# Where the gates of an interleaved scan are computed: in each group's own scan, or all ahead in the first

## The chip, the cores and the metric

The kernel runs on one core of one Trainium2 chip. A core has five engines that follow their own instruction streams: TensorE (PE in the profile, with its weight loads shown apart as PEld), VectorE (DVE), ScalarE (ACT), GpSimd (POOL) and SyncE (SP), which here only issues DMAs. The metric is the device time of one execution in microseconds (us). Lower is better. A profiled execution gives the trace; its span runs from the first to the last instruction.

## The reference, cut to what matters

The input `x` is 32 sequences of 256 tokens and 256 features. A gated state-space block (`_L0_cond_ref`) is followed by two layers of windowed attention with feed-forward (`_L0_ffn_ref`), and the input is added at the end. The change is in the first block:

```python
xr, gate = jnp.split(x @ W_in.T, 2, axis=-1)          # 512 channels each
xr = xr + t_emb[:, None, :]
xc = silu(conv4(xr) + b_conv)
xn = layernorm(xc) * ln_g + ln_b
Bm, Cm, dt = jnp.split(xn @ W_xproj.T, 3, axis=-1)
...
def step(h, inputs):                                    # one token after the other
    ad, bd, xt, ct = inputs
    h = jnp.clip(h * ad[:, :, None] + bd[:, :, None] * xt[:, None, :], -10.0, 10.0)
    return h, jnp.einsum('bd,bdh->bh', ct, h)
...
y = ys + D * xn
cond = y * jax.nn.silu(gate) @ W_out.T
...
out = x + ffn(cond)
```

All arithmetic is in float32.

## The kernel before

**Groups and slots.** The 32 sequences are four groups of 8 (`g` = 0 to 3 in the code; "groups 2 to 4" are `g` = 1 to 3). One group's scan is 256 steps, one per token, for all 8 sequences at once: a state tile `h` of 128 partitions (16 states x 8 sequences) by 512 channels is updated by one VectorE instruction (line 716). The scan is cut into 8 chunks of 32 steps (`c`, `CH` = 32). Work around the steps is put into numbered slots, one slot per step: `at(s, f, ...)` says that `f` is recorded in slot `s`, and `s0` is the first slot of a chunk. `scan_slots` runs through the slots and records what stands there. The scan of group `g` has the slots from 256·g on, so group 1 of the code is recorded right behind group 0.

**What runs with what.** The first scan (`alone`, `g` = 0) has the machine to itself. From slot 274 on, attention and feed-forward of group 0 are recorded, stage by stage, with the scan of group 1 between their stages, and so on: attention of group `g` runs beside the scan of group `g`+1. Attention and feed-forward of the last group run with no scan beside them. The tile framework builds the engines' instruction streams from the recorded order, its own estimates and the buffers that are free; each engine then runs its stream in order.

**One chunk of a scan.** `project` multiplies the chunk's inputs with `W_in`: one PSUM tile per 128 channels, two matmuls each (`KM` = 2 halves of the 256 features). Channels 0 to 3 are the convolution's inputs, channels `NC_` + 0 to 3 are the gates. For `g` = 0, `load_x` (line 452) loads the inputs and `project` (line 395, matmuls on line 399) makes all eight. For the later groups the four convolution inputs were made during the first scan: `ahead_load`, `ahead_project`, `ahead_copy`, `ahead_put` (lines 410 to 443) take 48 units `u`, each two of the channel tiles of one chunk, multiply, copy from PSUM on ScalarE and store to DRAM; `load_projected` (line 445) loads them back. Their gates were not: `load_x` and `project` run for them in each later scan, at slots `s0`+6 and `s0`+13 to `s0`+18.

**The gates.** `gate_th` (line 760) brings a gate tile from PSUM to SBUF in the order that the output needs (`reorder`, line 369). In the first scan it applies SiLU directly. In the later ones it copies, then takes tanh of half the value (line 768), and `gate_out` (line 771) forms (1 + tanh)·gate on VectorE, which is twice the SiLU. The factor is taken out by `halve` (line 327), which halves `W_out` once, and by `copy_y` (line 817), which doubles the first group's output. `out_gate` (line 790) multiplies with the gates at slots `s0`+25 and `s0`+41; `project_y` (line 805) applies `W_out`.

**The rows.** A step needs its token's normalised row on all 16 states, scaled per partition. `load_rows` (line 682) fetches it by a DMA that repeats the row 16 times from DRAM (`xrep<-xnd`, 256 KB), into one of 6 buffers, six slots ahead; `scale_row` (line 702) scales it on ScalarE two slots ahead. In the first scan some rows come from TensorE instead: `spread_rows` (line 687) makes two rows from `xq` by two matmuls that contract 32 partitions each, into two PSUM tiles (`bx`), and `scale_row` reads those. `by_tensor` (line 679) says which: with `NQ` = 4 and `XR` = 2, two rows of eight.

**Queues and buffers.** SP issues nearly all DMAs, in the recorded order. All PSUM tiles (`bank`) share 8 banks. The line numbers below are those of the kernel before.

Of the kernel before, what the change touches and what calls it, by code (L numbers as in the profile page):

```python
# [10 lines left out]
FP = mybir.dt.float32  # L11
BF = mybir.dt.bfloat16
I32 = mybir.dt.int32
AF = mybir.ActivationFunctionType
ALU = mybir.AluOpType
# [4 lines left out]
P = 128  # L20
# [6 lines left out]
GB = 8  # L27
# [46 lines left out]
def kernel(  # L74
# [147 lines left out]
    def program(ctx, exact):  # L222
# [14 lines left out]
        def constants(at):  # L237
# [88 lines left out]

            def halve():


                tc.keep_in_program_order(  # L330
                    nc.gpsimd.tensor_scalar_mul(w_out_sb, w_out_sb, 0.5)
                )

            def load_tables():
# [28 lines left out]
            at(-16, load_later)  # L363
            at(14, halve)
            at(30, load_tables)
# [11 lines left out]
        def group_scan(g):  # L377
# [32 lines left out]
            def ahead_load(u):  # L410
                if u % 2 == 0:
                    gg, c = 1 + u // 2 // NCH, u // 2 % NCH
                    t = ap_.tile([P, KM, GB, CH], FP, tag="rot", name="xa", bufs=4)
                    for k in range(KM):
                        nc.sync.dma_start(
                            out=t[:, k],
                            in_=xT[:, k, gg * GB : (gg + 1) * GB, c * CH : (c + 1) * CH],
                        )
                    state["xa", u // 2] = t

            def ahead_project(u):
                ps = bank(ps_w, "w", "ps_a").rearrange("p (r n) -> p r n", r=2)
                for r in range(2):
                    ch = 2 * (u % 2) + r
                    for k in range(KM):
                        nc.tensor.matmul(
                            ps[:, r],
                            w_in_sb[:, k, ch * P : (ch + 1) * P],
                            state["xa", u // 2][:, k],
                            start=(k == 0),  # L430
                            stop=(k == KM - 1),
                        )
                state["pa", u] = ps

            def ahead_copy(u):
                t = aw.tile([P, 2, GB * CH], FP, tag="pT", name="xs_a", bufs=6)
                nc.scalar.copy(t, state.pop(("pa", u)))
                state["ta", u] = t
# [6 lines left out]
            def load_projected(c, i):  # L445
                t = sp.tile([P, 2, GB * CH], FP, tag="xg", name="xp", bufs=2)
                nc.sync.dma_start(out=t, in_=projected[((g - 1) * NCH + c) * 2 + i])
                for r in range(2):
                    ck[c]["ps", 2 * i + r] = t[:, r]


            def load_x(c):
# [226 lines left out]
            def by_tensor(t):  # L679
                return alone and t % (2 * NQ) < XR  # L680

# [78 lines left out]
            def gate_th(c, ch):  # L760
                if ch == 0:
                    ck[c]["sg"] = sp.tile([P, NC_, GB * CH], FP, tag="sg", name="sg")
                sg = ck[c]["sg"][:, ch]
                reorder(sg, ck[c].pop(("ps", NC_ + ch)), AF.Silu if alone else AF.Copy)
                if alone:
                    return
                th = sp.tile([P, GB * CH], FP, tag="th", name="th_g", bufs=2)
                nc.scalar.activation(th, sg, AF.Tanh, scale=0.5)
                ck[c]["th_g", ch] = th

            def gate_out(c, ch):
                sg = ck[c]["sg"][:, ch]
                nc.vector.scalar_tensor_tensor(
                    sg, ck[c].pop(("th_g", ch)), 1.0, sg, ALU.add, ALU.mult
                )

# [40 lines left out]
            def copy_y(c, d):  # L817
# [6 lines left out]
                    AF.Copy,  # L824
                    scale=2.0 if alone else 1.0,
                )
# [29 lines left out]
            for c in range(NCH):  # L856
# [8 lines left out]
                for ch in range(NC_):  # L865
# [3 lines left out]
                    if not alone:  # L869
                        at(s0 - 35 + 2 * ch, conv_out, c, ch)  # L870
                for ch, s in enumerate((13, 16, 17, 18)):
                    at(s0 + s + 2, gate_th, c, ch)
                    if not alone:
                        at(s0 + s + 4, gate_out, c, ch)
                at(s0 - 25, raw_copy, c)
# [19 lines left out]
            for c in range(NCH):  # L895
                s0 = c * CH
                at(s0 - 43 if alone else s0 + 6, load_x, c)
                if alone:
                    for ch in range(NC_):
                        at(s0 - 40 + 2 * ch, project, c, ch)  # L900
                else:
                    for i in range(2):
                        at(s0 - 44 + 2 * i, load_projected, c, i)
                for ch, s in enumerate((13, 16, 17, 18)):
                    at(s0 + s, project, c, NC_ + ch)
                at(s0 - 27, raw_sums, c)
# [16 lines left out]
            if alone:  # L923
                n = (NG - 1) * NCH * 2
                for u in range(n):
                    s = -30 + u * (NCH * CH) // n
                    at(s - 5, ahead_load, u)
                    at(s, ahead_project, u)
                    at(s + 2, ahead_copy, u)
                    at(s + 4, ahead_put, u)  # L930
# [731 lines left out]
```

## Time and profile before

| What | Value |
|---|---|
| Median of three runs | 3590.94 us (3585.17 to 3603.19) |
| The profiled execution, its own time | 3582.75 us |
| Its span, first to last instruction | 3581.0 us |
| Busy share of the span | PE 96%, PEld 63%, DVE 74%, ACT 56%, POOL 53% |
| First step of the first scan (VectorE, line 716) | 47.53 us |
| Start of the second scan (line 836, second instruction) | 435.98 us |
| Mean granted clock of TensorE | 0.992 |
| DMA | 435.68 MB, 122 GB/s over the span |

Busy time is the time in which an engine executes at least one instruction. TensorE's matmuls overlap one another and their ends are modelled, so its busy time is not its work: two views are needed, how long it is busy and how closely instructions follow each other. A float32 matmul of the program appears as two records in the trace. A row of a group reads: line, engine, operation, tiles written and read, shapes, number of records, then busy us and mean ns of one, then the engine's idle time just before them and what ended it. A row of the windows view has the stretch, its length, then busy us and (number of instructions) for PE, PEld, DVE, ACT and POOL, the granted clock, the DMA engines' busy share and GB/s.

### The profile page before, as it was taken

The page shows a single profiled execution, that of the slowest core. Times are in us where ns is not written, and L with a number is a line of the kernel's source. Part 1 is how long each engine was busy: PE and PEld are TensorE (multiplying, and loading weights), DVE is VectorE, ACT ScalarE, POOL GpSimd, SP SyncE. Part 2 cuts the span into 40 slices and gives each one's busy share as a digit, 9 for nine tenths or more (in the row PEclk, how much of TensorE's full clock was granted, in tenths as well). Part 3 has the DMA queues.
Part 4 walks back from the last instruction along what each step waited for, and adds up shares of the span by engine and source line. Part 5 has one row for each costly group of instructions (what it writes and reads, how often), then busy time and mean ns, then how long its engine had stood idle before and what let it go on. Part 6 is the DMA issues. An engine that isn't in the chain of part 4 may idle for free.

```text
span 3581.0 us, 57673 instructions
## 1 busy us (share of the span) xinstructions
PE 3446.0 (96%) x20220; PEld 2253.9 (63%) x20220; DVE 2667.3 (74%) x5049; ACT 1998.7 (56%) x3599; POOL 1892.2 (53%) x1842
## 2 busy tenths in 40 slices
PE   7999989999999999999999999999999999999999
PEld 4555335666656666666666666666666677777777
DVE  5888889888788777888787778888877555555553
ACT  4666656656555665566566655655666444434442
POOL 4433477645556555655565556555544454544551
PEclk9999999999999999999999999999999999999999
DMA  7887665445354545444454555534454112011101
GB/s 207 219 221 213 198 174 149 120 117 143 109 144 125 149 141 148 130 118 127 118 142 125 138 149 140 143 106 131 114 141 122 54 50 61 13 30 38 33 27 37
DMA packets 468767, 435.68 MB, mean 122 GB/s; under 512 B 228723, under 2 KB 308084, under 8 KB 468340
## 3 DMA queue, kind: packets, MB, share of 16 engines
q1 hardware_dynamic: 384018, 419.88, 42.0%
q10 hardware_dynamic: 84450, 12.01, 2.0%
q8 instruction: 163, 2.67, 0.3%
q14 instruction: 136, 1.11, 0.1%
HBM read 383.54 MB, written 46.66 MB: 120 GB/s over the span
## 4 chain that ended last, share of the span: by engine, by line
PE 61%; DVE 19%; DMA 7%; POOL 6%; ACT 4%; issue 3%; SPq 0%; ACTq 0%; DVEq 0%; POOLq 0%
PE ps_qkv L989 13%; PE pa L1375 13%; DVE h L716 7%; PE po_f L1402 7%; DMA xrep<-xnd 5%; PE ps_wo L1039 5%; PE y L728 4%; PE ov L1271 4%; PE sc L1215 3%; PE ps_out L808 3%; PE ps_in L399 2%; PE tr_qk L1028 2%; PE rs L1252 2%; ACT xrep L706 2%; DVE acc L489 2%
## 5 line engine op out<-in xcount | busy, mean ns | idle before, releaser
L716 DVE CUSTOM_DVE_ANT_0 h<-h,xrep,lim 128x512 f32<-128x512 f32 x1024 | 961.0, 938 | 228.9 <-ACT xrep L706 196.6
L706 ACT ACTIVATE xrep<-xrep,beta 128x512 f32<-128x512 f32 x960 | 672.3, 718 | 341.4 <-DMA xrep<-xnd 219.8
L989 PE MATMUL ps_qkv<-qkv,res 128*128 128x512 f32 x1536 | 713.5, 601 | 17.9 <-DVE rinv L1260 8.4
L1375 PE MATMUL pa<-hT,w 128*128 128x256 f32 (+1 forms) x2816 | 675.1, 382 | 11.3 <-DVE zT L799 10.7
L1375 PEld LDWEIGHTS pa<-hT,w 128*128 128x128 f32 (+1 forms) x2816 | 516.9, 188 | 152.9 <-issue 35.4
L1013 POOL TENSOR_TENSOR rot<-rot,swp 128x512 f32<-128x512 f32 x256 | 339.9, 1328 | 475.3 <-DVE swp L1010 423.5
L1021 POOL TENSOR_TENSOR rn<-ss,neg_half 128x8 f32<-128x8 f32 x256 | 466.8, 1823 | 18.4 <-DVE ss L1019 7.8
L989 PEld LDWEIGHTS ps_qkv<-qkv,res 128*128 128x128 f32 x1536 | 282.2, 191 | 301.6 <-issue 241.4
L728 PE MATMUL y<-h,ly 128*32 128x512 f32 x2048 | 348.9, 609 | 16.9 <-DVE h L716 13.9
L1327 POOL TENSOR_TENSOR rstd<-ve,neg_half 128x2 f32<-128x2 f32 x64 | 46.9, 733 | 527.6 <-DVE ve L1325 511.3
L1393 DVE SCALAR_TENSOR_TENSOR ag<-pa,b_sb,ag 128x256 f32<-128x256 f32 x320 | 151.6, 474 | 222.4 <-ACT ag L1386 222.3
L1402 PE MATMUL po_f<-ag,w 128*128 128x256 f32 x1280 | 309.0, 389 | 5.9 <-DVE fo L1413 3.8
L1022 POOL TENSOR_TENSOR rot<-rot,rn 128x512 f32<-128x512 f32 x256 | 289.4, 1130 | 20.0
L1402 PEld LDWEIGHTS po_f<-ag,w 128*128 128x128 f32 x1280 | 236.8, 191 | 71.3 <-issue 12.0
L1386 ACT ACTIVATE ag<-pa,b_sb 128x256 f32<-128x256 f32 x320 | 150.2, 469 | 233.1 <-PE pa L1375 232.1
L1002 ACT ACTIVATE sq<-ps_qkv 128x512 f32<-128x512 f32 x256 | 150.8, 595 | 185.1 <-PE ps_qkv L989 119.4
L1039 PE MATMUL ps_wo<-oT,wo 128*128 128x256 f32 x1024 | 231.7, 379 | 0.5 <-DVE ag L1393 0.5
L489 DVE SCALAR_TENSOR_TENSOR acc<-xr,wc_sb,acc 128x256 f32<-128x256 f32 x384 | 195.1, 531 | 47.7 <-POOL acc L478 47.2
L1005 DVE TENSOR_TENSOR rot<-ps_qkv,rc_sb 128x512 f32<-128x512 f32 x256 | 174.8, 683 | 65.6 <-ACT sq L1002 65.0
L1039 PEld LDWEIGHTS ps_wo<-oT,wo 128*128 128x128 f32 x1024 | 194.4, 190 | 28.1 <-DVE ag L1393 0.9
L1227 ACT ACTIVATE pT<-sc 128x512 f32<-128x512 f32 x384 | 202.3, 603 | 7.6 <-PE sc L1215 5.8
L1271 PE MATMUL ov<-pT,v_sb 128*64 128x256 f32 (+1 forms) x2048 | 183.7, 330 | 19.4 <-DVE ag L1393 19.3
(160 smaller groups left out, 5482.8 us busy)
## 6 DMA issues: line engine op xcount, KB each, us to landing
xrep<-xnd SPq DMA_DIRECT2D x960, 256.0 KB
rb<-inv SPq DMA_DIRECT2D x128, 256.0 KB
xnd<-xn SPq DMA_DIRECT2D x64, 256.0 KB
qkv<-in_wqkv_dram SPq DMA_DIRECT2D x24, 512.0 KB
ahead<-xs_a SPq DMA_DIRECT2D x48, 256.0 KB
xp<-ahead SPq DMA_DIRECT2D x48, 256.0 KB
xd<-xnd SPq DMA_DIRECT2D x192, 64.0 KB
w<-in_w_dram SPq DMA_DIRECT2D x80, 128.0 KB
```

The costliest lines, as they stand in the source:

```text
L489: nc.vector.scalar_tensor_tensor(acc, xr[:, :, k : k + CH], wc_sb[:, ch, k : k + 1], acc, ALU.mult, ALU.add,)
L706: scaled = nc.scalar.activation(bx, ck[c].pop(("bx", t), bx), AF.Copy, scale=ck[c]["beta"][:, t : t + 1])
L716: nc.vector._custom_dve(TENSOR_ADD_SAT, out=h_new, in0=state["h"], in1=bx, s0=ck[c]["lim"][:, 0, t : t + 1], s1=ck[c]["lim"][:, 1, t : t + 1],
L728: nc.tensor.matmul(ck[c]["y", hb][32 * q : 32 * q + 32, :], ly[hb % 2][:, 32 * t : 32 * t + 32], ck[c].pop(("h", hb * TB + t)), start=(i = ...
L989: nc.tensor.matmul(ps, res[b][:, k, t0 : t0 + W], wt["qkv", a][:, k], start=(k == 0), stop=(k == KM - 1),)
L1013: nc.gpsimd.tensor_add(rot, rot, swp)
L1021: nc.gpsimd.tensor_tensor(rn, ss, neg_half, ALU.pow)
L1022: nc.gpsimd.tensor_mul(rot, rot, bc(rn, 2, DH))
L1039: nc.tensor.matmul(po[:, d], wt["wo", 0][:, c, d * P : (d + 1) * P], oT[:, c, :], start=(c == 0), stop=(c == NC_ - 1),)
L1271: nc.tensor.matmul(ov[r * DH : (r + 1) * DH, i, kw * W :], self.qkv[b][2][:, kw, h * DH : (h + 1) * DH], self.p.pop((b, kw, i0 + i, r)), s ...
L1375: nc.tensor.matmul(dst[x], wt["w1", m][:, k, x], self.h[:, k], start=(k == 0), stop=(k == KM - 1),)
L1402: nc.tensor.matmul(self.po[:, d], wt["w2", 0][:, m, d * P : (d + 1) * P], self.ag[m], start=(m == 0), stop=(m == len(MCH) - 1),)
```

## The change

The gates of groups 2 to 4 are made in the first scan as well. The units of `ahead_*` become 96: for each chunk two units of convolution inputs, as before, and two of gates, which are brought from PSUM by two SiLU instructions with the new order instead of one copy. They are stored in the same way, and `load_gates` loads them at slot `s0`+15. The units begin at slot −14 and spread over 276 slots (before: 48 units from slot −30 over 256). `load_x`, the gates' `project`, `gate_th` and `gate_out` are gone from the later scans; `halve` and the factor in `copy_y` are gone too. `by_tensor` now takes two rows of every four.

```diff
-            def halve():
-                tc.keep_in_program_order(
-                    nc.gpsimd.tensor_scalar_mul(w_out_sb, w_out_sb, 0.5)
-                )
...
-            at(14, halve)
...
             def ahead_load(u):
-                if u % 2 == 0:
-                    gg, c = 1 + u // 2 // NCH, u // 2 % NCH
+                if u % 4 == 0:
+                    gg, c = 1 + u // 4 // NCH, u // 4 % NCH
...
             def ahead_project(u):
...
-                    ch = 2 * (u % 2) + r
+                    ch = 2 * (u % 4) + r
...
             def ahead_copy(u):
                 t = aw.tile([P, 2, GB * CH], FP, tag="pT", name="xs_a", bufs=6)
-                nc.scalar.copy(t, state.pop(("pa", u)))
+                ps = state.pop(("pa", u))
+                if u % 4 < 2:
+                    nc.scalar.copy(t, ps)
+                else:
+                    for r in range(2):
+                        reorder(t[:, r], ps[:, r], AF.Silu)
                 state["ta", u] = t
...
-                nc.sync.dma_start(out=t, in_=projected[((g - 1) * NCH + c) * 2 + i])
+                nc.sync.dma_start(out=t, in_=projected[((g - 1) * NCH + c) * 4 + i])
...
+            def load_gates(c):
+                sg = ck[c]["sg"] = sp.tile([P, NC_, GB * CH], FP, tag="sg", name="sg")
+                for i in range(2):
+                    nc.sync.dma_start(
+                        out=sg[:, 2 * i : 2 * i + 2],
+                        in_=projected[((g - 1) * NCH + c) * 4 + 2 + i],
+                    )
...
             def by_tensor(t):
-                return alone and t % (2 * NQ) < XR
+                return alone and t % NQ < XR
...
-                sg = ck[c]["sg"][:, ch]
-                reorder(sg, ck[c].pop(("ps", NC_ + ch)), AF.Silu if alone else AF.Copy)
-                if alone:
-                    return
-                th = sp.tile([P, GB * CH], FP, tag="th", name="th_g", bufs=2)
-                nc.scalar.activation(th, sg, AF.Tanh, scale=0.5)
-                ck[c]["th_g", ch] = th
-
-            def gate_out(c, ch):
-                sg = ck[c]["sg"][:, ch]
-                nc.vector.scalar_tensor_tensor(
-                    sg, ck[c].pop(("th_g", ch)), 1.0, sg, ALU.add, ALU.mult
-                )
+                reorder(ck[c]["sg"][:, ch], ck[c].pop(("ps", NC_ + ch)), AF.Silu)
...
-                    scale=2.0 if alone else 1.0,
...
-                at(s0 - 43 if alone else s0 + 6, load_x, c)
                 if alone:
+                    at(s0 - 43, load_x, c)
...
+                    for ch, s in enumerate((13, 16, 17, 18)):
+                        at(s0 + s, project, c, NC_ + ch)
                 else:
                     for i in range(2):
                         at(s0 - 44 + 2 * i, load_projected, c, i)
-                for ch, s in enumerate((13, 16, 17, 18)):
-                    at(s0 + s, project, c, NC_ + ch)
+                    at(s0 + 15, load_gates, c)
...
-                n = (NG - 1) * NCH * 2
+                n = (NG - 1) * NCH * 4
                 for u in range(n):
-                    s = -30 + u * (NCH * CH) // n
+                    s = -14 + u * 276 // n
                     at(s - 5, ahead_load, u)
                     at(s, ahead_project, u)
                     at(s + 2, ahead_copy, u)
                     at(s + 4, ahead_put, u)
```

More of the change, by code (lines that the diff above doesn't have):

```diff
@@ L418, in ahead_load @@
                         )
-                    state["xa", u // 2] = t
+                    state["xa", u // 4] = t
             def ahead_project(u):
@@ L428, in ahead_project @@
                             w_in_sb[:, k, ch * P : (ch + 1) * P],
-                            state["xa", u // 2][:, k],
+                            state["xa", u // 4][:, k],
                             start=(k == 0),
@@ L870, in group_scan @@
                         at(s0 - 35 + 2 * ch, conv_out, c, ch)
-                for ch, s in enumerate((13, 16, 17, 18)):
-                    at(s0 + s + 2, gate_th, c, ch)
-                    if not alone:
-                        at(s0 + s + 4, gate_out, c, ch)
+                if alone:
+                    for ch, s in enumerate((13, 16, 17, 18)):
+                        at(s0 + s + 2, gate_th, c, ch)
                 at(s0 - 25, raw_copy, c)
@@ L896, in group_scan @@
                 s0 = c * CH
-                at(s0 - 43 if alone else s0 + 6, load_x, c)
                 if alone:
+                    at(s0 - 43, load_x, c)
                     for ch in range(NC_):
                         at(s0 - 40 + 2 * ch, project, c, ch)
+                    for ch, s in enumerate((13, 16, 17, 18)):
+                        at(s0 + s, project, c, NC_ + ch)
                 else:
@@ L903, in group_scan @@
                         at(s0 - 44 + 2 * i, load_projected, c, i)
-                for ch, s in enumerate((13, 16, 17, 18)):
-                    at(s0 + s, project, c, NC_ + ch)
+                    at(s0 + 15, load_gates, c)
                 at(s0 - 27, raw_sums, c)
```

## The prediction

> **What bounds the kernel now.** I read the windows view first, by stage: four middle chunks of the first scan, the stage in which attention runs beside a scan, and the last stage, in which no scan is left.
>
> ```profile
> core 0: us, PE busy (x) PEld busy (x) DVE busy (x) ACT busy (x) POOL busy (x), PEclk, DMA share, GB/s
> 149.50:341.20 191.70, 182.45 (x806) 97.32 (x805) 168.45 (x293) 126.47 (x233) 73.94 (x98) 0.97 0.82 220
> 1000.00:2500.00 1500.00, 1453.63 (x9025) 963.51 (x9024) 1205.73 (x2307) 899.74 (x1639) 878.06 (x833) 1.00 0.49 134
> 3000.00:3500.00 500.00, 500.00 (x2928) 361.41 (x2928) 273.90 (x544) 211.63 (x360) 244.72 (x201) 1.00 0.12 32
> ```
>
> Beside a scan TensorE is busy 97% of the time and VectorE 80%; with no scan TensorE is busy throughout. So both later stages are TensorE's, and work taken from it there comes back as time. The first scan is less plain: TensorE 95%, VectorE 88%, the DMA engines 82%, at 47.9 us a chunk (191.70 / 4). Whether TensorE has room there decides the case, and its busy time cannot tell. So next the timeline of TensorE in one chunk (start, length, what, count):
>
> ```profile
> 357.69 1.13 PE L693 MATMUL bx<-xq,rep_w 32*128 32x512 f32 x4
> 358.75 1.99 PE L426 MATMUL ps_a<-xa,w_in_sb 128*128 128x256 f32 x8
> 360.67 1.06 PE L728 MATMUL y<-h,ly 128*32 128x512 f32 x8
> 361.67 1.99 PE L808 MATMUL ps_out<-zT,w_out_sb 128*128 128x256 f32 x8
> 363.50 1.89 PE L399 MATMUL ps_in<-xg,w_in_sb 128*128 128x256 f32 x8
> 365.32 1.06 PE L728 MATMUL y<-h,ly 128*32 128x512 f32 x8
> ...
> 379.51 3.26 PE L728 MATMUL y<-h,ly 128*32 128x512 f32 x8
> 383.81 1.04 PE L728 MATMUL y<-h,ly 128*32 128x512 f32 x2 [1.03 <-DVE h L716]
> ```
>
> Packed, each group starts when the one before ends: 1.92 us for eight `ps_a` records (360.67 − 358.75), 1.0 us for eight `y`, 1.06 us for four `bx`. Near the chunk's end the same eight `y` take 3.26 us, since they wait one by one for `h`; that counts as busy. The waits and the chain of waits in the same four chunks say what else holds the scan:
>
> ```profile
> ACT xrep L706 <- DMA xrep<-xnd: 41.2, 38, 3.8
> PEld y L728 <- DVE h L716: 10.0, 17, 1.7
> ...
> by line: DMA xrep<-xnd 24.3%; DVE h L716 20.1%; PE y L728 8.1%; ACT xrep L706 7.6%; issue 7.1%; PE ps_a L426 4.7%; PE ps_raw L518 3.7%; POOL acc L478 3.7%; PE ps_in L399 3.5%; DMA xq<-xnd 2.8%; PE bx L693 2.3%; DVE acc L489 2.3%; PE ps_out
> ```
>
> Rows that come late by DMA are a quarter of the chain; VectorE's steps a fifth; TensorE's lines share much of the rest. It is a mixture, with TensorE not yet the one bound.
>
> **TensorE's real load in a chunk of the first scan.** By count times packed spacing: 64 `y` records 8.0 us; 48 `ps_a` 11.5; 32 `ps_in` 7.5; 16 `ps_out` 3.7; 16 `bx` 4.2; `ps_raw`, the two transposes and `ps_st` together 4.6 (1.0, 0.5, 0.45 and 0.5 us for four in the same timeline). Sum 39.5 of 47.9 us: 82%, with 8.4 us free.
>
> [...] The row has matmuls busy 182.45 of 191.70 us and weight loads 97.32. [...]
>
> **Part 1: what the later scans lose.** 3 groups x 8 chunks x 4 gate tiles x 2 halves = 192 matmuls, 384 records. The rows of the groups view, for 1000 to 2500 us:
>
> ```profile
> L399 PE MATMUL ps_in<-xg,w_in_sb 128*128 128x256 f32 x240 | 61.0, 386 | 0.0
> L371 ACT ACTIVATE sg<-ps_in 128x256 f32<-128x256 f32 x60 | 38.9, 652 | 19.8 <-PE ps_in L399 19.8
> L773 DVE SCALAR_TENSOR_TENSOR sg<-th_g,sg 128x256 f32<-128x256 f32 x60 | 26.7, 444 | 19.9 <-ACT th_g L768 19.9
> L768 ACT ACTIVATE th_g<-sg 128x256 f32<-128x256 f32 x60 | 25.0, 416 | 1.3
> ```
>
> 61.0 / 240 gives 0.254 us a record, packed spacing 0.24: 384 x 0.24 = 92 us of TensorE. Also gone are 192 ScalarE instructions (96 x (0.652 + 0.416) = 103 us) and 96 on VectorE (96 x 0.444 = 43 us); both engines have 20% and more free there, so I count these at nothing. Since TensorE is busy 97%, I take −92 us. Bounds: −70, if a quarter of the work stood where TensorE would have waited anyway; −110, if its waits shrink in proportion with the relief of the other two.
>
> What comes in: 48 loads of 256 KB (`load_gates`) for 48 of 128 KB, on SP. The new load is recorded at slot `s0`+15 behind the row loads up to that slot, and waits for the `sg` of the chunk before, last read at its `s0`+41, six slots earlier. Behind it on SP wait row loads, and for those ScalarE; but a row load itself waits for a buffer that a step six rows back frees, so SP is no further ahead than VectorE by then. The gates are needed ten slots later, some 30 us at this stage's pace, against row transfers of 4 to 6 us in the chain. DMA is 49% busy. Zero; if SP were held, rows would come late there and VectorE after them.
>
> **Part 2: what the first scan gets.** Units: 96 over 276 slots is 11.1 a chunk, not 6, each 8 records: +5.1 x 1.92 = +9.9 us. Rows: 8 more a chunk, 4 pairs of 1.06 us: +4.2 us. TensorE's load becomes 53.6 us a chunk against 47.9 now, so it becomes the bound. In six middle chunks the floor is 6 x 5.7 = +34 us. It will not be packed perfectly, as `y` waits for `h` in the stretch with the convolution. I take 96% (the later stage reaches 97% busy with VectorE at 80%): 53.6 / 0.96 = 55.8, +7.9 a chunk, +47 for six. The first chunk gets +3, the last +2, as the old units ended at 386 us and left TensorE room (340 records from 341 to 437 us against 806 in twice that). At the start two input tiles and four stores fewer stand in SP's queue ahead of the first chunk's rows, and all of the first layer's weights instead of two thirds, about as many bytes: nothing. Sum +52 us. Bounds: +34 at full packing; +80 at 90% packing (59.6 a chunk, +70 for six, and more at the ends).
>
> The other engines: ScalarE gets 48 x 2 SiLUs, 11 a chunk at 0.655 us, the price of the same operation in the first scan's `sg` row: +7.3 on 31.6 us a chunk, 70% of the new length. It frees the `ps_a` banks, two slots later as before. VectorE keeps 42.1 us. DMA: 64 row loads fewer (−16.8 MB), 48 stores more (+12.6 MB): the 41.2 us of waiting for rows shrink, but the room goes to TensorE. On SP a store waits for two SiLUs instead of one copy, and row loads stand behind it; they are issued six slots early, so 0.7 us more is covered. `halve` (one instruction on POOL) is nothing.
>
> **Sum.** −92 + 52 = −40 us, on the profiled execution's 3582.75 us (span 3581.0): 3543. The median shown lies 8.2 us above that execution, so 3590.94 − 40 = 3551. The likeliest case reaches from −76 (−110 + 34) to −18 (−92 and a first scan at 91% packing, +74): 3515 to 3573.
>
> **Rivals.**
> A. The first scan hardly grows. For it: rows by DMA are 24% of the chain, and they are halved. Against: 53.6 us of load in 47.9. Below its floor it would need denser packing than in the timeline. With −100 and +20: 3511.
> B. TensorE is not what the later scans wait for. For it: VectorE is 80% busy, and its `h` steps 446 us of that. Against: 97% and the last stage's 100%. Half of the 92 us is lost to other waits: −46 + 52, 3597, no change.
> C. Slower: the first scan keeps the packing it has now. Rows from TensorE queue behind units, ScalarE and the step come late, `y` waits for the step, and the next rows wait behind `y` on the same engine. At today's 82%: 53.6 / 0.82 = 65.4 a chunk, +17.5 for six and some +15 at the ends: +120, and −92: 3619. It decides from a chunk of about 60.5 us on, where the growth eats the 92. For it: eight `y` that take 3.26 us. Against: a spread row is recorded four slots and a read-out two slots away from its step, some 10 us in all against one ScalarE instruction (0.7) and one step (0.95).
> D. The change doing less than it says is excluded for its counts; they follow from the code.
>
> **How the numbers follow.** About 0.5% (18 us, the spread of the three runs) is what a measurement can tell from no change. Likeliest case 0.53, A 0.17, B 0.13, C 0.17. Faster by over 0.5%: the first two, 0.70; within: B and a little of C, 0.14; slower 0.16. The range leaves out C's far end and A's: 3506 to 3604.
>
> **What would show it.** Right: chunks of the first scan of 54 to 58 us, so that the second scan starts near 488 us and not 436; TensorE gapless in them; waits of ScalarE for rows by DMA under 10 us in four chunks; from there to the end about 92 us less. Wrong: a first scan with long `y` groups and idle stretches on TensorE (C); a later part that shrinks by under 60 us (B); waits for `sg` or for late row loads in the later scans.

## The result: slower

The changed kernel takes 3676.36 us in the median of four runs (3674.76 to 3679.27), beside 3588.06 us for four runs of the kernel before: a ratio of 1.0239, 95% interval 1.0208 to 1.0269. 3551 was forecast. In the two profiled executions the span went from 3581.0 to 3672.8 us, by 91.8 us. The steps of the scans, one VectorE instruction each, cut this difference into parts:

| Part | Before, us | After, us | Difference | Predicted |
|---|---|---|---|---|
| To the first step of the first scan | 47.5 | 55.6 | +8.1 | 0 |
| First scan, first step to the second scan's first | 389.1 | 495.5 | +106.4 | +52 |
| Scans of groups 2 to 4 | 2359.1 | 2336.4 | −22.7 | −92 |
| From the last step to the end | 785.2 | 785.3 | +0.1 | 0 |

Both large terms failed. Six middle chunks of the first scan take 63.1 us each (48.2 before, 55.8 predicted). The windows view of the changed kernel (stretch, its length, then busy us and count by engine, the granted clock, the DMA engines' share and GB/s) shows the four middle chunks of the first scan and the stage of attention beside a scan:

```profile
core 0: us, PE busy (x) PEld busy (x) DVE busy (x) ACT busy (x) POOL busy (x), PEclk, DMA share, GB/s
180.20:428.20 248.00, 229.01 (x1041) 134.04 (x1040) 158.95 (x291) 145.01 (x274) 74.98 (x98) 0.95 0.57 153
1100.00:2600.00 1500.00, 1429.16 (x8879) 931.39 (x8880) 1198.86 (x2263) 855.98 (x1529) 878.85 (x839) 0.99 0.49 138
```

TensorE has 1041 records where it had 806, but in 248.0 us, not in the 214 that 53.6 us a chunk would be. Its busy share fell from 95% to 92%, VectorE's from 88% to 64%, and the DMA engines' from 82% to 57%: no engine is fuller than before, and the chunk is a third longer. In the later stage TensorE's share fell from 97% to 95%; most of the relief was not turned into time. The waits of the same four chunks (engine, line, tile; us in total, times, longest):

```profile
POOL xd L762 <- PE tz L777: 62.2, 8, 14.8
DVE h L720 <- ACT xrep L710: 56.4, 19, 5.7
ACT xrep L710 <- DMA xrep<-xnd: 54.4, 34, 4.7
```

ScalarE waited 41.2 us for rows by DMA before, and 54.4 now that a third fewer rows come that way; the steps on VectorE wait 56.4 us for ScalarE. The timeline of one such stretch shows the loop (start, length, engine, line, what; in brackets the idle time before it and what ended it):

```profile
338.53 0.72 ACT L710 ACTIVATE xrep<-xrep,beta 128x512 f32<-128x512 f32 x1 [2.14 <-DMA xrep<-xnd]
339.60 0.72 ACT L710 ACTIVATE xrep<-xrep,beta 128x512 f32<-128x512 f32 x1 [0.35 <-DMA xrep<-xnd]
340.23 1.11 ACT L363 ACTIVATE xs_a<-ps_a 128x256 f32<-128x256 f32 x2
341.12 0.70 ACT L363 ACTIVATE sg<-ps_in 128x256 f32<-128x256 f32 x1
341.36 0.32 SPq L439 DMA_DIRECT2D ahead<-xs_a  x1
...
341.39 2.65 PE L418 MATMUL ps_a<-xa,w_in_sb 128*128 128x256 f32 x8 [1.96 <-ACT xs_a L363]
341.60 1.23 ACT L710 ACTIVATE xrep<-bx,beta 128x512 f32<-128x512 f32 x2
341.78 1.22 SPq L689 DMA_DIRECT2D xrep<-xnd  x2
342.28 0.81 DVE L720 CUSTOM_DVE_ANT_0 h<-h,xrep,lim 128x512 f32<-128x512 f32 x1 [5.62 <-ACT xrep L710]
342.71 1.14 ACT L363 ACTIVATE xs_a<-ps_a 128x256 f32<-128x256 f32 x2
...
346.09 0.72 ACT L710 ACTIVATE xrep<-xrep,beta 128x512 f32<-128x512 f32 x1 [2.24 <-DMA xrep<-xnd]
```

Read it from the top. ScalarE scales two rows that came by DMA, then applies SiLU to two tiles of a unit and to a gate, and only then scales the two rows that TensorE spread (341.60); VectorE's step has waited 5.62 us for the first of them. SP issues the store of the unit when its SiLU is done (341.36), and behind it in its queue the next two row loads (341.78). After two more SiLUs (342.71) ScalarE's next instruction is the scaling of the first of these rows; it waits 2.24 us for the row and starts at 346.09, 4.3 us after the loads were issued, in front of the scaling of the next rows from TensorE. From 338.53 to 346.09 one turn for four rows takes 7.56 us; eight such turns would be 60.5 us, near the 63.1 us of a chunk.

### The profile page after: what moved, and what is told of

Its sections match the earlier page's. It is cut to its first block, busy times and chain, and to the rows that moved or that the text cites. A ratio compares the mean times of both kernels' runs of the same rounds, so it can differ in the third digit from the quotient of the medians.

```text
span 3672.8 us, 57737 instructions
## 1 busy us (share of the span) xinstructions
PE 3480.8 (95%) x20348; PEld 2276.8 (62%) x20348; DVE 2613.8 (71%) x4953; ACT 1957.3 (53%) x3503; POOL 1882.3 (51%) x1841
## 4 chain that ended last, share of the span: by engine, by line
PE 50%; DVE 19%; POOL 11%; DMA 9%; ACT 6%; issue 4%; SPq 1%; ACTq 0%; DVEq 0%; POOLq 0%
PE pa L1366 11%; PE ps_qkv L980 11%; DVE h L720 7%; DMA xrep<-xnd 7%; PE po_f L1393 6%; PE ps_wo L1030 4%; PE ov L1262 3%; PE sc L1206 3%; PE y L732 3%; POOL rn L1012 2%; DVE acc L493 2%; ACT xrep L710 2%; PE ps_a L418 2%; PE tr_qk L1019 2%; PE rs L1243 2%
## 5 line engine op out<-in xcount | busy, mean ns | idle before, releaser
L710 ACT ACTIVATE xrep<-xrep,beta 128x512 f32<-128x512 f32 x896 | 624.0, 719 | 433.1 <-DMA xrep<-xnd 304.7
L980 PE MATMUL ps_qkv<-qkv,res 128*128 128x512 f32 x1536 | 721.0, 606 | 40.1 <-DVE xd L771 11.9
L732 PE MATMUL y<-h,ly 128*32 128x512 f32 x2048 | 306.6, 609 | 16.8 <-DVE h L720 15.5
L493 DVE SCALAR_TENSOR_TENSOR acc<-xr,wc_sb,acc 128x256 f32<-128x256 f32 x384 | 181.6, 491 | 46.1 <-POOL acc L482 45.3
L418 PE MATMUL ps_a<-xa,w_in_sb 128*128 128x256 f32 x768 | 200.8, 408 | 8.0 <-ACT raw L530 3.6
```

The costliest lines, as they stand in the source:

```text
L418: nc.tensor.matmul(ps[:, r], w_in_sb[:, k, ch * P : (ch + 1) * P], state["xa", u // 4][:, k], start=(k == 0), stop=(k == KM - 1),)
L493: nc.vector.scalar_tensor_tensor(acc, xr[:, :, k : k + CH], wc_sb[:, ch, k : k + 1], acc, ALU.mult, ALU.add,)
L710: scaled = nc.scalar.activation(bx, ck[c].pop(("bx", t), bx), AF.Copy, scale=ck[c]["beta"][:, t : t + 1])
L732: nc.tensor.matmul(ck[c]["y", hb][32 * q : 32 * q + 32, :], ly[hb % 2][:, 32 * t : 32 * t + 32], ck[c].pop(("h", hb * TB + t)), start=(i = ...
L980: nc.tensor.matmul(ps, res[b][:, k, t0 : t0 + W], wt["qkv", a][:, k], start=(k == 0), stop=(k == KM - 1),)
```

## The experiments

All measured against the kernel before in the same job; times are medians, the parts come from one profiled execution each. "Chunk" is the mean of six middle chunks of the first scan; ratios stand with their 95% interval where there were enough runs.

| Kernel | us | Ratio | First step | First scan | Chunk | Scans of groups 2 to 4 |
|---|---|---|---|---|---|---|
| before | 3588 to 3598 | | 47.5 | 389.1 | 48.2 | 2359.1 |
| after | 3676.36 | 1.0239 [1.0208, 1.0269] | 55.6 | 495.5 | 63.1 | 2336.4 |
| e1 half of the rows only | 3639.88 | 1.0123 [1.0099, 1.0147] | 50.5 | 435.0 | 55.7 | 2368.7 |
| e2 gates only | 3641.54 | 1.0132 [1.0112, 1.0152] | 55.0 | 459.0 | 58.4 | 2338.2 |
| e3 after, stores by ScalarE | 3650.75 | 1.0156 [1.0139, 1.0173] | 53.2 | 465.7 | 58.6 | 2343.8 |
| e4 before without later gates | 3580.38 | 0.9961 [0.9946, 0.9976] | 51.4 | 392.3 | 48.6 | 2342.7 |
| e5 e1, buffers split | 3640.77 | one run | 48.7 | 425.6 | 54.0 | 2379.5 |
| e6 e1, stores by ScalarE | 3640.13 | one run | 50.9 | 435.7 | 56.0 | 2365.3 |
| e7 before, half of the later gates' matmuls | 3590.56 | 0.9983 [0.9966, 0.9999] | 49.1 | 394.2 | 48.9 | 2361.8 |
| e8 e1, row order kept | 3599.81 | one run | 51.0 | 390.2 | 49.4 | 2371.5 |
| e9 after, row order kept | 3613.83 | 1.0045 [1.0028, 1.0062] | 55.8 | 425.8 | 52.7 | 2344.5 |
| e10 e9, stores by ScalarE | 3617.21 | 1.0047 [1.0028, 1.0066] | 52.8 | 433.5 | 54.2 | 2343.1 |
| e11 before, fewer later taps | 3568.91 | 0.9918 [0.9887, 0.9949] | 50.8 | 392.6 | 48.5 | 2339.3 |
| e12 before, row order kept | 3618.07 | 1.0058 [1.0040, 1.0077] | 52.2 | 411.5 | 51.8 | 2367.4 |
| e13 e4 and e11 together | 3562.78 | 0.9922 [0.9905, 0.9938] | 52.7 | 390.1 | 47.7 | 2331.0 |
| e14 e2, row order kept | 3601.33 | 1.0029 [1.0016, 1.0042] | 56.9 | 423.1 | 53.1 | 2333.6 |
| e15 e4, later norm's pair left out | 3527.85 | 0.9799 [0.9776, 0.9822] | 47.1 | 389.1 | 48.8 | 2307.1 |
| e16 before, later norm's pair left out | 3585.68 | 0.9966 [0.9951, 0.9982] | 49.5 | 389.3 | 48.8 | 2363.5 |
| e17 e14, that pair on VectorE | 3588.95 | 0.9977 [0.9964, 0.9990] | 59.4 | 422.1 | 53.3 | 2320.0 |
| e18 e14, half of that pair on VectorE | 3600.26 | 1.0011 [0.9999, 1.0022] | 54.4 | 425.3 | 53.2 | 2332.8 |

How far a difference in the last column can be trusted, the table tells itself: six kernels whose later scans are those of before (before, e1, e5, e6, e8, e12) have 2359 to 2380 us there, mean 2368.6; seven with the gates gone from the later scans and nothing else (after, e2, e3, e4, e9, e10, e14) have 2334 to 2345, mean 2340.3. So the gates' removal is worth 28 us there, and differences of under some 10 us say nothing.

### The first scan: one part at a time

e1 is the kernel before with one line of the change, e2 the change without that line:

```diff
 # e1                                       # e2 is the reverse in the changed kernel
-                return alone and t % (2 * NQ) < XR
+                return alone and t % NQ < XR
```

> Half of the first scan's rows by TensorE, nothing else changed. Theory (the growth of the first scan comes from the 96 stores of projected tiles, which stand in SP's queue ahead of row loads and wait there for ScalarE): this part is harmless, a chunk of the first scan stays at 46 to 49 us (now 48.2), time 3570 to 3595 us. Rival (TensorE bounds the first scan at the 86% packing seen in the changed kernel): the load of 43.7 us a chunk over 0.86 gives 50.8 us a chunk, +20, 3610 us.

> The gates are made ahead as in the changed kernel, but a quarter of the rows is spread by TensorE as before. Theory of the stores: more rows wait behind the stores, so a chunk is 62 to 66 us, as long as in the changed kernel or longer, time 3670 to 3710 us. Rival (TensorE): its load falls to 49.4 us a chunk, at 86% packing 57.5, that is 4.5 us a chunk less than in the changed kernel, 3640 us.

Each part alone makes the first scan longer, by 46 and 70 us; together it is 106. In e1 TensorE's load is 39.5 + 4.2 = 43.7 us of a chunk of 55.7, so its load is not what costs there, and neither theory had so long a chunk. In e2 the number of the rival came (57.5 us a chunk, 3640 us), but its reason, TensorE at 86% packing, does not fit e1, where the packing would be 78%.

### Two suspects: the stores and the row buffers

In e3 and e6 the stores of the units are issued by ScalarE; in e5 the six row buffers are split, four for rows by DMA and two for rows from TensorE.

```diff
 # e3, e6 (and e10, below)
-                nc.sync.dma_start(out=d, in_=state.pop(("ta", u)))
+                nc.scalar.dma_start(out=d, in_=state.pop(("ta", u)))
 # e5
+            def row_tile(main):
+                tag, bufs = ("xrep", 4) if main else ("xrep2", 2)
+                return xp.tile([P, DI], FP, tag=tag, name="xrep", bufs=bufs)
```

> The changed kernel with the 96 stores issued by ScalarE behind its own copies, not by SP. Theory of the stores: row loads no longer wait behind them, a chunk of the first scan falls from 62 to 54 to 57 us, ScalarE's waits for rows shrink by half, time 3620 to 3640 us. Rival (TensorE bound at 86% packing): chunk 61 to 63 us, time within 10 us of 3676.

> Half of the rows by TensorE alone (that run: 55.4 us a chunk of the first scan, 3640 us), with the six row buffers split: four for rows by DMA, two for rows by TensorE, which so can no longer take a buffer that a load needs. Theory of the buffers (spread rows take them early and hold loads back): chunk 49 to 52 us, 3590 to 3615 us. Rival (ScalarE's and VectorE's static orders wait for one another whatever the buffers): chunk 54 to 57 us, 3630 to 3650 us.

> Half of the rows by TensorE alone, with the 48 stores issued by ScalarE and not by SP. Theory of the stores (they hold row loads back in SP's queue; in that run SP waited 44 us in four chunks for their copies): chunk 50 to 52 us instead of 55.4, 3600 to 3615 us. Rival (static order): 54 to 57 us a chunk, 3630 to 3650 us.

Without SP's wait for the SiLU the changed kernel wins 26 us, 30 in the first scan, between what the two theories gave: the store in front of the row loads is a link of the loop above, but not the loop. With half of the rows alone, neither edit moves the time (3640 in both, one run each). The split buffers make the first scan 9 us shorter and the later ones, which they also touch, 11 us longer; they were not tried in the changed kernel.

### ScalarE's order

Only in the later scans does the kernel keep the row scalings in the recorded order; in the first the framework is free to put them elsewhere in ScalarE's stream. e8, e9 and e12 take that freedom away, in e1, in the changed kernel and in the kernel before; e10 is e9 with the stores by ScalarE.

```diff
-                if not alone:
-                    tc.keep_in_program_order(scaled)
+                tc.keep_in_program_order(scaled)
```

> Half of the rows by TensorE alone, with the first scan's row scalings kept on ScalarE behind what is recorded before them, as the later scans have it; only ScalarE's order changes. Theory of the static order (the order that the framework chose for ScalarE puts row scalings where they block the chunk's normalisation, and the other way round): the chunk changes by more than 2 us from 55.4 with the same work, to 49 to 53 if the recorded order is the better one. Rivals of buffers or stores: 54 to 57 us a chunk.

> The changed kernel, with the first scan's row scalings kept on ScalarE behind what is recorded before them. Theory of the static order (half of the rows alone cost 45 us by it and lost them again when pinned): a chunk of the first scan falls from 62 us to 54 to 58, the time from 3676 to 3620 to 3645 us. Rival (order matters only without the gates; here TensorE's 53.6 us a chunk and the stores decide): 60 to 63 us a chunk, 3660 to 3680 us.

> As the run before, and the 96 stores issued by ScalarE instead of SP. If SP's waits for the copies cost by themselves (with the unpinned order they cost 26 us): chunk 53 to 56 us, 3605 to 3630 us, and clearly below the pinned kernel. If they were an effect of the order: within 8 us of the pinned kernel.

> The control: the kernel before with the first scan's row scalings pinned, a quarter of the rows by TensorE. If pinning undoes a damage that half of the rows brought: within 10 us of the kernel before. If pinning is a gain of its own that hid a loss by the rows: 3550 to 3575 us.

That is the cause of most of it. One line, with no work more or less, takes 40 us from e1 (in one run; its first scan falls from 435.0 to 390.2) and 62 from the changed kernel.

What the free order does can be counted in the traces, if the scalings are matched to the rows by their order. Of every four rows in the changed kernel the first two come from TensorE and the other two by DMA, and the steps use them in this order. In 55 of the 64 fours of its first scan ScalarE scales both rows by DMA before the first of the two from TensorE; in e3 in 38, in e1 in 19, in e8, e9 and e10 in none. With two rows of eight from TensorE, the two rows behind them go ahead in 18 of 32 eights in e2, and in none in the kernel before, in e12 and in e14. So ScalarE stands waiting for a transfer in front of rows that are needed sooner. The line moves a little more than ScalarE's stream: in the first scans of the changed kernel and of e9 TensorE's instructions stand in the same order, but VectorE's, GpSimd's and SP's differ in places too, and no run takes these apart.

The waits of ScalarE in the first scan of e9, 160 to 370 us:

```profile
ACT xc L503 <- DVE acc L493: 24.1, 16, 2.0
ACT sq_x L597 <- POOL xn L591: 10.7, 8, 2.0
ACT ad L647 <- DVE bcd L636: 6.8, 4, 1.9
ACT xs_a L431 <- PE ps_a L418: 5.5, 5, 1.7
...
ACT xrep L710 <- DMA xrep<-xnd: 0.6, 1, 0.6
```

The wait for rows by DMA, 54.4 us in four chunks of the changed kernel, is down to 0.6. And the four middle chunks of e9 in the windows view:

```profile
161.30:370.20 208.90, 208.90 (x1043) 127.19 (x1042) 161.18 (x293) 145.24 (x276) 71.01 (x98) 1.00 0.68 182
```

TensorE has no idle time in 208.90 us, 52.2 us a chunk. That is the floor, counted as 53.6: these chunks of e9 are held by TensorE's load, and its first scan is 36.7 us longer than before. e10 shows that the stores no longer matter then (1.0047 against 1.0045). e12 is the control, and neither of its two expectations came: in the kernel before the same line costs 22 us of the first scan. Keeping the recorded order is no gain in itself; the freely made order fitted the old mixture of work and not the new one.

e14 is e2 with that line, the gates without the additional rows:

> The changed kernel with a quarter of the first scan's rows by TensorE, as before, and with the first scan's row scalings kept in the recorded order on ScalarE. TensorE's load in a chunk of the first scan is 39.5 + 9.9 = 49.4 us. If the order of ScalarE is what cost in the kernel with gates alone (3642 us, 58 us a chunk), this gives 51 to 53 us a chunk and 3590 to 3615 us; if the load of TensorE were all that counts with the order kept, 50 us a chunk and 3585 to 3595, level with the kernel before; if the order is not what cost without the additional rows from TensorE (the same pin made the kernel before slower by 0.6%), 57 us or more and 3635 to 3660.

53.1 us a chunk, at the upper end of the 51 to 53 us of the first case, and as long as e9's 52.7: with the order kept, the additional rows from TensorE neither help nor cost beside the gates. TensorE's load is 49.4 us here, so its load does not hold e14 alone; what else does was not followed up.

### The later scans: who holds them

The 28 us are not spread evenly. The scan of group 2 takes 735 to 742 us in the six kernels with the gates and 743 to 749 in the seven without, 7 us more in the mean; the scans of groups 3 and 4 are 19 and 16 us shorter. In the scan of group 2 ScalarE waits longer for rows by DMA, first the kernel before, then the changed one, over that scan:

```profile
ACT xrep L706 <- DMA xrep<-xnd: 55.8, 33, 5.8
ACT xrep L710 <- DMA xrep<-xnd: 99.5, 48, 7.8
```

In e4, whose first scan is that of before, it is 106.6 us. All seven kernels load the gates, or in e4 other tiles in their place (`load_gates`, 48 loads on SP in the rows' queue); none leaves these loads out, so whether they make the rows late is open.

e4 leaves the later gates out of the kernel before, e7 half of their matmuls, e11 two of the three additions of the later convolutions, e13 does e4 and e11 together.

```diff
 # e4
-                for ch, s in enumerate((13, 16, 17, 18)):
-                    at(s0 + s, project, c, NC_ + ch)
+                if alone:
+                    for ch, s in enumerate((13, 16, 17, 18)):
+                        at(s0 + s, project, c, NC_ + ch)
+                else:
+                    at(s0 + 15, load_gates, c)
 # e7
-                for k in range(KM):
+                n = KM if alone else KM // 2
+                for k in range(n):
 # e11
-                for k in range(1, TAPS):
+                for k in range(1, TAPS if alone else 2):
```

> The kernel before, with the gates of groups 2 to 4 left out: no input loads, matmuls, tanh and products for them, and the stored convolution inputs loaded in their place, unactivated, so those groups' outputs are not the reference's. The first scan is as before. If the later scans are TensorE's, this gives the 92 us of the prediction: 3490 to 3505 us. If only part of it comes back there whatever the first scan does: 25 to 45 us, 3545 to 3565 us. If the poor 25 us in the changed kernel came from what its first scan left behind, this one shows the 92.

> The kernel before, with the gates of groups 2 to 4 made from one half of the input features: one of the two matmuls of each is left out (96 of 192, 46 us of TensorE's time), so those groups' outputs are not the reference's. All else, waits and the other engines' work, stays. If the later scans are bound by TensorE: −46 us, 3545 us. If not: −15 to +5 us, 3575 to 3595 us.

> The kernel before, with two of the convolution's three later taps left out in groups 2 to 4: 192 VectorE instructions of 0.53 us, 102 us of VectorE's time, about as much as the gates took of TensorE's; those groups' outputs are not the reference's. If VectorE holds the later scans: −60 us and more, below 3535 us. If no engine's load does by itself (TensorE's half gave 5 us of 46): 0 to −30 us, 3565 to 3595 us.

> The kernel before, with both reliefs at once: the later gates are left out (TensorE -92 us, ScalarE -103, VectorE -43; stored convolution inputs are loaded in their place), and two of the three additions of the convolution in groups 2 to 4 are left out (VectorE -102). Alone they gave about -14 and -27 us. Theory T (TensorE and VectorE hold the later scans together: when one is relieved the other sets the pace): both at once give clearly more than the sum, under 3525 us. Theory O (each engine waits in its own fixed order, and a relief only shortens those waits that happen to lie on it): the two add, 3545 to 3560 us. Theory N (something that neither touches, such as the chain from step to step, holds the pace): less than the sum, above 3565 us.

e4 gives 14 us in the time, less than either of its expectations. 46 us of TensorE taken away (e7) are not to be told from nothing in the later scans (2361.8), and the time fell by 0.17%, its interval just clear of 1. 102 us of VectorE (e11) give 29 us there, as much as all the gates on three engines. So TensorE alone does not hold these scans, though it is busy 97% of them. In the waits of TensorE from 1500 to 2500 us, first of the changed kernel, then of e7, the time appears as waits for VectorE and ScalarE; all idle time of TensorE there sums to 26.3 us in the kernel before, 37.4 in the changed one and 42.4 in e7:

```profile
PE ps_qkv L980 <- DVE xd L771: 9.6, 12, 1.4
PE tr_qk L1019 <- DVE rinv L1251: 9.2, 7, 1.4
PE ps_qkv L980 <- ACT oT L1269: 5.3, 7, 1.2
```

```profile
PE ov L1272 <- DVE ag L1394: 12.3, 9, 1.4
PE pa L1376 <- DVE zT L800: 10.1, 9, 2.1
PE ps_qkv L990 <- DVE rinv L1261: 5.6, 8, 0.9
```

Both reliefs at once (e13) gave 38 us in those scans, less than the sum of 28 and 29, and in the time no more than e11 alone. In microseconds it lies between theory O's end and theory N's, and theory T is out: TensorE and VectorE do not hold the scans between them. What may be left shows in the chain of waits of e13 (start, length, what; pieces of under 0.15 us between the lines are left out), over 20 us of one chunk in which TensorE is not in the chain until its end:

```profile
1714.28 0.96 POOL stat L573
1715.26 0.30 ACT stat L580
1715.59 0.79 ACT xn L587
1716.44 1.29 POOL xn L594
1717.81 1.28 POOL xn L595
1719.11 0.73 ACT sq_x L601 x2
1719.87 0.18 DVE ss L607
1720.12 0.71 POOL stat L608
1720.82 1.35 POOL acc L486 x2
...
1728.76 0.73 DVE h L724
1729.54 4.15 DMA xrep<-xnd
1733.78 0.72 ACT xrep L714
1734.50 0.48 ACT qT L1043
1735.02 1.13 PE ps_qkv L999 x2
```

The normalisation of the next chunk's rows goes back and forth between GpSimd and ScalarE, a convolution behind it and a step wait for it, a row's buffer and so its transfer wait for the step, ScalarE's scaling for the transfer, and attention's matmuls for a copy behind that scaling. e15 and e16 leave out the two GpSimd instructions `xn` of this chain in groups 2 to 4, without and with the gates:

```diff
                 xn = ck[c]["xn", j]
+                if not alone:
+                    return
                 nc.gpsimd.tensor_mul(xn, xn, lng_sb)
                 nc.gpsimd.tensor_add(xn, xn, lnb_sb)
```

> The kernel before without the later gates (TensorE -92 us, ScalarE -103, VectorE -43), and in groups 2 to 4 also without the two GpSimd instructions that apply the layer norm's factor and offset to the rows (48 pairs of some 2.8 us, 134 us of GpSimd). Without the gates alone: 3580 us. Theory G (once TensorE is relieved, a chain through ScalarE, VectorE, GpSimd and a row's transfer sets the pace, and these two instructions stand in it once a chunk): 1.5 to 3 us a chunk less, 24 chunks, 3500 to 3545 us. Theory N (no engine's work matters any more, the order does): 3570 to 3590 us.

> The kernel before, gates kept, without those two GpSimd instructions in groups 2 to 4 (134 us of GpSimd). If TensorE with its 97% sets the pace as long as the gates are there: no change, 3585 to 3597 us. If the chain through the other engines sets part of the pace in the kernel before too: 3545 to 3575 us, and the relief of GpSimd is worth more than that of TensorE (-5 us for 46, -14 for 92).

e15 is theory G's. With the gates kept, the pair is worth 5 us in the later scans, less than the column can tell (2363.5 against a mean of 2368.6); the time is 0.34% lower, its interval clear of 1. With the gates gone, it is worth 33 us (2307.1 against 2340.3). Together the two reliefs give 61 us where the single ones give 28 and 5, and a ratio of 0.9799 where they give 0.9961 and 0.9966: more than the sum. The gates' work and this pair hold the later scans side by side, and whichever is taken away, the other is met a little later. Which part of the gates' work it is, on TensorE, ScalarE or VectorE, is not shown: all three are taken away together, and half of TensorE's part alone (e7) was worth nothing that can be told.

### A version without leaving work out

e17 and e18 are e14 with this pair, or its addition alone, on VectorE in groups 2 to 4.

```diff
+                e = nc.gpsimd if alone else nc.vector
-                nc.gpsimd.tensor_mul(xn, xn, lng_sb)
-                nc.gpsimd.tensor_add(xn, xn, lnb_sb)
+                e.tensor_mul(xn, xn, lng_sb)     # e18: nc.gpsimd
+                e.tensor_add(xn, xn, lnb_sb)
```

> The changed kernel with a quarter of the rows by TensorE and the row scalings of the first scan kept in the recorded order (3601 us, ratio 1.0029), and in groups 2 to 4 the layer norm's factor and offset applied by VectorE instead of GpSimd; all of the computation is there. With those two instructions gone altogether and the gates gone the scans of groups 2 to 4 became 52 us shorter than in the kernel before, and 16 with the gates alone. Theory G (what lay in the way was the 2.8 us of GpSimd in the chain): VectorE does the pair in some 1.3 us (its additions of 128x512 stand at 0.6 to 0.7 us), so about half of the 35 us is won, less some 5 to 10 us for 62 us more of VectorE work: 3575 to 3595 us, level with or faster than the kernel before. Rival V (VectorE, 80% busy, is in the chain as much as GpSimd is, as -29 us for 102 us of its work showed): the gain is eaten, 3600 to 3620 us.

> As the run before, with only the addition of the offset on VectorE and the factor left on GpSimd; all of the computation is there. Theory G: half of that gain, 3585 to 3600 us. Rival V: 3597 to 3612 us.

In e17 the later scans fall by another 14 us against e14 and by 49 against the mean of the kernels with the gates in place; the time is 0.23% below the kernel before, its interval just clear of 1, and some 2.5% below the changed kernel's. The groups view of VectorE, 1500 to 2500 us, has the pair (row as in the tables of before: count | busy us, mean ns | idle before):

```profile
L591 DVE TENSOR_TENSOR xn<-xn,lng_sb 128x512 f32<-128x512 f32 x20 | 18.1, 904 | 18.0 <-ACT xn L583 16.4 <-DMA xrep<-xnd 1.6
L592 DVE TENSOR_TENSOR xn<-xn,lnb_sb 128x512 f32<-128x512 f32 x20 | 13.8, 688 | 0.3
```

By their means 1.59 us, where GpSimd took 2.57 in the chain above. The gain is theory G's. e17 does not show that moving the gates pays: the kernel before with this pair on VectorE and nothing else changed was not run, and e16, the gates in place and the pair left out, is 0.34% below the kernel before. Half of the pair (e18) does nothing that can be told in those scans (2332.8 against 2333.6); its 3600.26 us lies where the two theories overlap.

## Why the prediction was wrong

**The floor of the first scan: right.** TensorE's load was put at 53.6 us a chunk; with the order kept, TensorE is gapless at 52.2 in four chunks (e9). Six middle chunks grow by 27 us, where the floor was +34; the whole first scan grows by 36.7, since its last chunk takes 58.0 us where it took 47.2. A chunk that long was to be had.

**The packing: wrong, and the larger miss of the first scan.** "I take 96%" packing was taken from a stage with other work and another order. The changed kernel has 52.2 / 63.1 = 83%. The text had the price of this: rival C, "keeps the packing it has now", 65.4 us a chunk and +120. C's size was nearly right (63.1 and +106), and its mechanism half: the row from TensorE does stand behind the units on ScalarE and the step waits for it, but the wait that closes the loop is not `y` before the next rows on TensorE; it is ScalarE waiting for a row by DMA in front of the rows from TensorE, as the timeline and the counts show. The argument against C counted one scaling and one step against slots of room, as if ScalarE ran in the order of the slots. In the first scan it does not: the framework orders it, and a change of the mixture makes another order. The value of e12 against e8 and e9 is in this: the same line costs 22 us before and wins 40 and 62 after.

**Costs put at nothing.** "0.7 us more is covered" for the store on SP: without the store there the changed kernel is 26 us faster (e3, which takes away the whole wait and not the 0.7 us alone), so the store was not covered; with the order kept it is (e10). "Nothing" for the start: the first step came 8.1 us later, and 5 to 12 us later in all kernels with gates ahead (52.8 to 59.4, against 47.1 to 52.7 in the others). Two things were seen together and not told apart: other loads in front, and in the changed kernel and in e9 a granted TensorE clock of 0.85 instead of 1.00 over the first 45 us. "Waits of ScalarE for rows by DMA under 10 us": 54.4 in the changed kernel, 0.6 in e9.

**The later scans: wrong by 64 to 70 us, the largest miss.** "Work taken from it there comes back as time" was read from a busy share of 97%. Of 92 us, 23 to 28 came back. Busy time counts matmuls that wait one by one for their operands, as the eight `y` of 3.26 us did, and half of the gates' matmuls were worth nothing that can be told (e7). Rival B was the right kind, with too small a loss and only one partner: it had VectorE as the one that is waited for and half of the 92 lost; about 70% were lost. Of this loss some 33 us came back when the pair on GpSimd was left out as well (e15 against e4 and e16); where the other half went, in it the 7 us by which the scan of group 2 grew, stays open. That the other engines' relief counts "at nothing" was wrong as well: 102 us of VectorE, at 80% busy, gave 29 us.

**Right, and half right.** The tail did not move. No wait for `sg` stands among the waits of 1100 to 2600 us, so the gates come in time; but one sign named for a wrong prediction, late row loads in the later scans, was there in the scan of group 2 (99.5 us of ScalarE's waits, 55.8 before), so that the loads cost nothing is not shown.

**Weight loads and TensorE's room.** In e9 the weight loads' busy share is 127.19 / 208.90 = 61% (97.32 / 191.70 = 51% before) in a stretch where TensorE has no gap, and the chunk is 4.5 us longer than before: a share of weight loads far below 100% did not show that TensorE had room here. Counting matmuls by their packed spacing gave the chunk's length to 3% (53.6 against 52.2 us).

**The sum.** −92 + 52 was forecast, and −22.7 + 106.4 + 8.1 came. Of the first scan's miss of 54 us, all goes with the order: e9 is below the 52 forecast. What is not settled: why the framework puts the rows by DMA first, where the other half of the later scans' loss went, and why the first step is late.

## What to carry to other kernels

A busy share of 97% did not mean here that work taken away comes back (92 us of TensorE's were worth 28, half of them nothing that can be told): leave out a part of the work on one engine, then on two, before moving it at a cost elsewhere; if two reliefs together give more than their sum, as 61 us against 28 and 5 here, both limits lie close together and both must be moved. When work is added to a stage whose stream a framework orders, count the load for the floor, and price the order separately: the same work took 52.7 or 63.1 us a chunk. Look on each engine for an instruction that waits for a transfer in front of work that others wait for.

## What was not expected of the hardware

TensorE's granted clock was at half for 60 us of the span in the kernel before (mean 0.992) and for 142 us in the changed one (0.981), in stretches of 3.4 and 6.8 us mostly. That is up to 41 us more of TensorE's time lost, an estimate (half of the 82 us), with hardly more matmuls in sum (those of the additional spread rows). In the middle chunks of the first scan the clock and TensorE's idle time were 0.97 with 9.3 us idle of 191.7 (before), 0.95 with 19.0 of 248.0 (after), 1.00 with none of 208.9 (e9); but also 0.96 with 22.7 of 223.6 (e1), more idle time and a higher clock than in the changed kernel, so the sum of the idle time does not set the clock alone. Whether a gap on TensorE is paid for a second time by the clock was not shown: no run changed the clock alone, and how much of the 106 us of the first scan it is was not measured.
